# Step sizes by ScalarE's softplus between two table loads, and more products with C on VectorE, in a Mamba-style block with attention

## The chip, the cores and the metric

One NeuronCore of one Trainium2 chip runs the whole program. The metric is the device time of one execution in microseconds (us). The five engines run their own instruction streams in order: TensorE (PE in the profile), VectorE (DVE), ScalarE (ACT), GpSimd (POOL) and SyncE (SP), whose queue issues the DMAs. They wait for each other on semaphores.

## What is computed

The input is eight images of 96 channels by 64 by 64 points. For each image the reference does a layer norm, a projection to 192 channels, a depthwise convolution and a SiLU; then four selective scans over 4096 points each (two orders of reading the image, each forwards and backwards); then a norm, a gate, a projection, two 3x3 convolutions with GELU, an attention without softmax and a small feed-forward net. The change lies in the scans, cut here to what matters:

```python
delta = softplus(dts + dt_projs_b)            # step sizes, 192 channels x 4096 points, for each of 4 directions
def step(hst, inp):                           # hst: 192 channels x 16 states
    u_i, dt_i, b_i, c_i = inp
    dA = exp(dt_i[..., None] * A)             # decays
    hst = dA * hst + (dt_i * u_i)[..., None] * b_i
    y = einsum('bkdn,bkn->bkd', hst, c_i)     # products with C, summed over the 16 states
    return hst, y
```

## The kernel before

**Units and slots.** The scans are cut into 256 units: 8 images x 4 directions x 8 chunks of T = 512 points. A unit holds 192 channels x 16 states x 512 points, as 24 tiles of 128 x 512. They are worked in 24 slots, six groups n = 0 to 5 of four slots each. Per slot, ScalarE makes one tile of decays into PSUM (`decays`, L1123, an Exp), and VectorE runs one scan instruction over 512 points (L1195). `decays(q + 2)` is issued in slot q, so the decays of a slot are issued two slots ahead of its scan. Four PSUM banks hold decays. GpSimd makes the inputs of a whole group at once (`inputs`, L998, 128 x 2048: step size times u, times B). TensorE sums the products over the states (`sums`, L1024).

**Products with C.** Where a slot is "banked", the scan is written over its decays in PSUM, and VectorE multiplies it by C in a further instruction (L1201), issued after the next slot's scan; ScalarE copies the last column as the carry (L1202). In the other slots the scan is written over the inputs in SBUF; ScalarE copies the carries of the whole group at once after its last slot (L1207), and GpSimd multiplies what is not banked of the group by C (`outputs`, L1004). `BANKED` (L34) gives how many of the four slots of each group are banked: (4, 0, 4, 0, 4, 2) in 56 units, (4, 0, 4, 0, 4, 3) in 200.

**Step sizes.** `step_sizes` (L953) makes softplus(x) = max(x, 0) + ln(1 + exp(-|x|)) in steps: the matmul that makes x in PSUM (L963), then Abs, Exp and Ln on ScalarE (L971, L973, L975), then maximum and sum on VectorE (L977), then step size times u on GpSimd (L980). One unit needs one such tile for channels 0 to 127 ("a"), and two neighbouring units share one for channels 128 to 191 ("b"), so two units need three. They are made one unit ahead or two, in slots written out by hand in `plan` (L1057): tile "a" in slots 6, 8, 9, 10, 11 and 12 of each unit, tile "b" in slots 9, 11, 12, 13, 15 and 16 of each odd unit. The PSUM banks "y01" and "y2" hold x, and also the sums over the states; `gather` (L1038) empties them by ScalarE in slots 3 and 7.

**Side streams.** Beside the scans of image b, the front of image b + 1 and the back end of image b - 1 advance by one step per slot or so (`Stream`, `advance`); their ScalarE, VectorE and TensorE instructions stand between those of the slots, in the order in which they are issued. SiLU and GELU need another activation table than Exp and Ln: `table` (L274) issues an ACT_TABLE_LOAD before and after them. `quiet` lets them in only in the slots listed in `CALM` (L267).

Within a slot the order of issue is: carry copies left from the slot before; decays of two slots on; the scan; the product of the slot before; the steps that `plan` put there; the side streams. Every engine works through its own share of that order.

Of the kernel before, what the change touches and what calls it, by code (L numbers as in the profile page):

```python
# [9 lines left out]
F32 = mybir.dt.float32  # L10
F16 = mybir.dt.float16
F8 = mybir.dt.float8e5
AF = mybir.ActivationFunctionType
ALU = mybir.AluOpType
# [5 lines left out]
B, C, HW = 8, 96, 64  # L20
L = HW * HW
DI, N, R = 192, 16, 6
T = 512
NC = L // T
G = 4
# [3 lines left out]
W2 = HW + 2  # L29
# [1 line left out]
SPREAD = 5  # L31
HB = 6

BANKED = ((4, 0, 4, 0, 4, 2), (4, 0, 4, 0, 4, 3))  # L34

HOLD = 3
LAND = 11
# [6 lines left out]
def kernel(ctx: ExitStack, tc: tile.TileContext, a, out):  # L44
# [8 lines left out]
    nc = tc.nc  # L53
    P = 128
# [8 lines left out]
    def bank(tag, name):  # L63
        return psum.tile([P, T], F32, tag=tag, name=name, bufs=BANKS[tag])
# [11 lines left out]
    one = const([P, 1], 1.0, "one")  # L76
# [110 lines left out]
    def back_kit(pool, tag, extra, other=None, upper=0):  # L187

        k = Kit()
        k.tag, k.solo, k.upper = tag, not extra, upper  # L190
        if other is None:
            k.ya, k.za, k.bs, k.r, k.d1, k.s1, k.s2, y, z = (plain(pool, f"{tag}b{i}") for i in range(9))
            k.pad = padded(pool, tag + "pad")
        else:
            k.ya, k.za = (x.t for x in other.x)
            k.bs, k.r, k.d1, k.s1 = other.e
            k.s2, y, z = (other.pre[:, i, :] for i in range(3))
            k.pad = other.pad
        k.yb, k.zb = Part(y), Part(z[64:P])
        k.ya, k.za, k.bs = Part(k.ya), Part(k.za), Part(k.bs)  # L200
        if pool is None:
            return k
        k.t2 = Part(k.r), k.ya
        k.ln = Part(pool.tile([C + 1, T], F32, name=tag + "ln"))
        nc.gpsimd.memset(k.ln.t, 1.0)
        k.im = other.im if other else Part(pool.tile([C + 1, 18, W2], F32, name=tag + "im"))
        k.m3 = [Part(pool.tile([C, 8, W2], F32, name=f"{tag}m3{i}")) for i in range(2)]
        k.gm = gm0 if not extra else pool.tile([P, 8, W2], F32, name=tag + "gm")
        if extra:
            nc.gpsimd.memset(k.gm, 0.0)  # L210
        k.x8 = pool.tile([C, T], F8, name=tag + "x8")
        k.h16 = pool.tile([P, 3, T], F16, name=tag + "h16")
        k.h8 = pool.tile([P, 3, T], F8, name=tag + "h8")
        k.o16 = pool.tile([C, T], F16, name=tag + "o16")
        return k
# [9 lines left out]
    def square(ap):  # L225
        return ap.rearrange("p (r w) -> p r w", r=8)
# [37 lines left out]

    alone = [False]
    place = [None]
    CALM = (0, 1, 8, 9, 16, 17)  # L267

    def quiet():

# [3 lines left out]
    def table(name):  # L274
        nc.scalar.preload_act_table_set(name)  # L275
# [457 lines left out]
    units, images = [], []  # L733
    for b in range(out.shape[0]):

        s = {"b": b, "done": set(), "live": b + 1 == out.shape[0], "pairs": (1, 0) if b else (0, 1)}
        images.append(s)
        for order, (pair, back) in enumerate((p, k) for p in s["pairs"] for k in range(2)):
            for i in range(NC):
                u = Unit()  # L740
                u.s, u.pair, u.back, u.k = s, pair, back, pair + 2 * back
                u.c, u.start = (NC - 1 - i if back else i), i == 0
                u.order, u.new, u.i = order, (order, i) == (0, 0), len(units)
                u.bc, u.hb, u.delta, u.du, u.p = {}, {}, {}, {}, {}
                u.banked = BANKED[int(b == 0 or u.i % 32 >= NC)]
                units.append(u)

    TILES = [(g, j) for g in range(2) for j in range(3)]
# [3 lines left out]
    first = front(0, images[0])  # L752
# [10 lines left out]
    dt_w = wp.tile([P, 3, 64], F32, name="dt_w")  # L763
# [161 lines left out]
    def states(u, what, g):  # L925

        t = sp.tile([P, G, T], F32, tag="bc"[what], name="bc"[what])
        r0 = u.back * (XD // 2) + what * N + g * 2 * G
        src = u.s["xd"][u.pair][u.c, r0 : r0 + 2 * G, :].rearrange("(h m) l -> h (m l)", h=2)
        for h in range(2):  # L930
            to = t[64 * h : 64 * h + 64].rearrange("p m l -> p (m l)")
            nc.sync.dma_start(to, src[h].unsqueeze(0).to_broadcast([64, G * T]))
        u.bc[what, g] = t
# [16 lines left out]
        for h, w in enumerate((u, v)):  # L950
            nc.sync.dma_start(u.ub[64 * h : 64 * h + 64], w.s["u"][w.pair][P:DI, bass.ts(w.c, T)])

    def step_sizes(us, i):  # L953

        u, which = us[0], "ab"[len(us) - 1]
        if i == 0:
            u.ps = bank("y01" if which == "a" else "y2", "dt")
            if which == "a":
                todo = [(u.ps, slice(0, P), u)]
            else:  # L960
                todo = [(u.ps[64 * h : 64 * h + 64], slice(P, DI), w) for h, w in enumerate(us)]
            for ps, d, w in todo:
                nc.tensor.matmul(ps, dt_w.rearrange("r j d -> r (j d)")[32 * w.k : 32 * w.k + R + 1, d], w.dts, start=True, stop=True)  # L963
            u.nat = sp.tile([P, T], F32, tag="nat" + which, name="nat", bufs=1)
            if which == "a":
                u.nata = u.nat
            else:
                for w in us:
                    w.natb = u.nat
        elif i == 1:  # L970
            nc.scalar.activation(u.nat, u.ps, AF.Abs)  # L971
        elif i == 2:
            nc.scalar.activation(u.nat, u.nat, AF.Exp, scale=-1.0)  # L973
        elif i == 3:
            nc.scalar.activation(u.nat, u.nat, AF.Ln, bias=one)  # L975
        elif i == 4:
            nc.vector.scalar_tensor_tensor(u.nat, u.ps, 0.0, u.nat, ALU.max, ALU.add)  # L977
        else:
            x = u.ua if which == "a" else u.ub
            nc.gpsimd.tensor_tensor(x, u.nat, x, ALU.mult)  # L980

    def spread(u, what, js):

# [16 lines left out]
    def outputs(u, n):  # L1000

        lo = u.banked[n]
        hb = u.hb[n][:, lo:, :]
        nc.gpsimd.tensor_tensor(hb, hb, u.bc[1, TILES[n][0]][:, lo:, :], ALU.mult)  # L1004

# [51 lines left out]
    def plan(u, last, nxt, third, fourth):  # L1057

        at = [[] for _ in range(24)]

        def put(slot, f, *args):
            at[slot].append((f, args))

        if last:
            put(0, outputs, last, 5)
            for m in range(2):
                put(m, sums, last, (3, 4), 2 + m)
            for m in range(2):
                put(3 + m, sums, last, (5,), m)
            put(3, gather, last, 0)  # L1070
            put(7, states, u, 1, 1)
            put(7, gather, last, 1)
        for n in range(6):
            to = (u, n + 2) if n < 4 else (nxt, n - 4)
            if to[0]:
                put(4 * n + 1, inputs, *to)
        if third and u.i % 2:
            put(16, step_sizes, (nxt, third), 5)
        put(8, outputs, u, 1)
        put(16, outputs, u, 3)  # L1080
        for m in range(4):
            put(13 + m, sums, u, (0, 1), m)
            if m < 2:
                put(18 + m, sums, u, (2,), m)
                put(22 + m, sums, u, (3, 4), m)
        put(18, before, u)
        if nxt:
            put(0, spread, nxt, 0, (0, 1))
            put(1, spread, nxt, 1, (0, 1))
            put(10, states, nxt, 0, 0)  # L1090
            put(15, states, nxt, 1, 0)
            put(20, states, nxt, 0, 1)
            if u.i % 2 == 0:
                put(15, spread, nxt, 0, (2,))
                put(16, spread, nxt, 1, (2,))
        if third:
            if third.i < NC:
                put(0, fetched_dt, third)
            put(5, fetched_u, third)
            for i, slot in enumerate((6, 8, 9, 10, 11, 12)):  # L1100
                put(slot, step_sizes, (third,), i)
            if u.i % 2:
                for i, slot in enumerate((9, 11, 12, 13, 15)):
                    put(slot, step_sizes, (nxt, third), i)
                put(17, spread, nxt, 0, (2,))
                put(18, spread, nxt, 1, (2,))
            elif u.i + 3 < len(units):
                put(21, fetched_pair, third, units[u.i + 3])
        if fourth and fourth.i >= NC:
            put(14, fetched_dt, fourth)  # L1110
        return at

    def at_index(i):
# [16 lines left out]
    fetched_u(units[0])  # L1130
    fetched_pair(*units[:2])
    states(units[0], 0, 0)
    for us, js in ((units[:1], (0, 1)), (units[:2], (2,))):
        for i in range(6):
            step_sizes(us, i)
        for what in range(2):
            spread(units[0], what, js)
    for what, g in ((1, 0), (0, 1), (1, 1)):
# [3 lines left out]
    inputs(units[0], 1)  # L1142
    decays(0)
    decays(1)
    for i in range(6):
        step_sizes(units[1:2], i)

    def advance(n):

# [4 lines left out]
    for u in units:  # L1154
        last, nxt, third, fourth = (at_index(u.i + d) for d in (-1, 1, 2, 3))
        if u.new:
            drained(*side)
            b = u.s["b"]
# [25 lines left out]
        for slot in range(24):  # L1184
            n, m = divmod(slot, G)
            g, j = TILES[n]
# [21 lines left out]
                )  # L1208
            for f, args in todo[slot]:
                f(*args)  # L1210
            place[0] = slot
            advance(slot)
    place[0] = None
    if product:
# [88 lines left out]
```

## Time and profile before

| | |
|---|---|
| median of 3 runs | 10769.33 us (10765.02 to 10771.17) |
| the profiled execution's own time | 10764.72 us |
| its span | 10763.0 us |
| first scan starts, last scan ends | 181 us, 10533 us |
| VectorE busy | 10158.1 us (94%) |
| GpSimd busy | 10118.0 us (94%) |
| TensorE busy | 8423.7 us (78%) |
| ScalarE busy | 7397.8 us (69%) |

An engine's busy time is the union of its instructions: neighbours overlap a little, so that the pitch from one start to the next is shorter than an instruction's duration. L12 is line 12 of the kernel. In a group of instructions the name before the arrow is what is written, the names behind it what is read; `x384` is the count; after it come the busy time in us, the mean ns of one, and after the bar the engine's idle time just before such instructions, with what ended most of it.

### The profile page before, as it was taken

Reading aid. Unit: us, or ns where it says so; the run is one execution under the profiler, and the core shown is the slowest. Engines: PE = TensorE matmul, PEld = TensorE weight load, DVE = VectorE, ACT = ScalarE, POOL = GpSimd, SP = SyncE. Lnnn points to the kernel's source line nnn. Section 1 sums busy time; section 2 is a strip of 40 time slices with the busy share of each in tenths; the row PEclk is TensorE's granted clock in tenths of the full one; section 3 lists DMA queues with packets and bytes.
Section 4 is the critical chain, followed back from the end, with each engine's and each line's share of the span. In section 5 each row is a group of like instructions: output and inputs, shape, how many; then the busy total and the mean of one; then the engine's idle time right before and its main releaser. Section 6 shows DMA issues by size and latency. Waiting matters only on the chain. (4 is left out here: it accounts for less than half of the span.)

```text
span 10763.0 us, 97608 instructions
## 1 busy us (share of the span) xinstructions
PE 8423.7 (78%) x23270; PEld 2274.2 (21%) x23270; DVE 10158.1 (94%) x11126; ACT 7397.8 (69%) x15154; POOL 10118.0 (94%) x2782
## 2 busy tenths in 40 slices
PE   7777668886788867888688886888768887677677
PEld 2121112221122211222122221222112221111112
DVE  3999999999999999999999999999999999999993
ACT  4666666777676776777767776677766767666674
POOL 3999999999999999999999999999999999999991
PEclk8888788987889878998789887898778987778788
DMA  6888888998889988898888988889888898888883
GB/s 148 208 205 209 200 209 214 226 226 200 215 216 227 227 193 220 216 231 219 201 218 214 237 212 202 217 220 237 198 211 218 219 235 200 202 203 210 208 214 94
DMA packets 1095381, 2253.29 MB, mean 209 GB/s; under 512 B 435993, under 2 KB 436698, under 8 KB 963731
## 3 DMA queue, kind: packets, MB, share of 16 engines
q1 hardware_dynamic: 1094803, 2247.05, 84.5%
q8 instruction: 184, 3.01, 0.1%
q14 instruction: 394, 3.23, 0.1%
HBM read 1507.14 MB, written 336.69 MB: 171 GB/s over the span
## 5 line engine op out<-in xcount | busy, mean ns | idle before, releaser
L998 POOL TENSOR_TENSOR hb<-b,du 128x2048 f32<-128x2048 f32 x1536 | 6952.6, 4546 | 6.1 <-DMA du<-ua 5.2
L1024 PE MATMUL p<-hb,halves 128*64 128x512 f32 x12288 | 3713.8, 707 | 1053.0 <-POOL hb L1004 562.6
L1123 ACT ACTIVATE da<-delta,w_a_logs 128x512 f32<-128x512 f32 x6144 | 4164.3, 689 | 541.5 <-DVE hb L1195 447.5
L1195 DVE TENSOR_TENSOR_SCAN da<-da,carry,hb 128x512 f32<-128x512 f32 x3311 | 4164.0, 1274 | 90.7 <-ACT carry L1202 37.0
L1004 POOL TENSOR_TENSOR hb<-hb,c 128x2048 f32<-128x2048 f32 (+2 forms) x768 | 2714.3, 3534 | 222.3 <-ACT carry L1207 203.0
L1195 DVE TENSOR_TENSOR_SCAN hb<-da,carry,hb 128x512 f32<-128x512 f32 x2065 | 2547.0, 1265 | 1.8
L1201 DVE TENSOR_TENSOR hb<-da,c 128x512 f32<-128x512 f32 x3784 | 2534.0, 670 | 1.8 <-DMA c<-xd 0.9
L1202 ACT COPY carry<-da 128x1 f32<-128x1 f32 x3784 | 593.8, 157 | 2054.5 <-DVE hb L1201 2045.1
L1024 PEld LDWEIGHTS p<-hb,halves 128*64 128x64 f32 x12288 | 904.8, 157 | 3697.8 <-issue 1876.0
L313 PE MATMUL conv<-f0im,taps 97*128 97x512 f32 (+1 forms) x2088 | 867.7, 655 | 37.2 <-ACT f0pre L369 32.2
L1195 DVE TENSOR_TENSOR_SCAN da<-da,hb 128x512 f32<-128x512 f32 x473 | 566.1, 1214 | 28.0 <-POOL hb L998 26.6
L963 PE MATMUL dt<-dts,dt_w 7*128 7x512 f32 (+1 forms) x1024 | 485.9, 742 | 92.3 <-ACT carry L1207 36.2
L980 POOL TENSOR_TENSOR ua<-nat,ua 128x512 f32<-128x512 f32 x256 | 329.9, 1289 | 170.9 <-DVE nat L977 161.8
L313 PEld LDWEIGHTS conv<-f0im,taps 97*128 97x128 f32 (+1 forms) x2088 | 256.4, 173 | 588.2 <-issue 508.8
L1207 ACT COPY carry<-hb 128x4 f32<-128x4 f32 (+2 forms) x768 | 149.7, 195 | 302.1 <-DVE hb L1195 293.7
L1195 DVE TENSOR_TENSOR_SCAN hb<-da,hb 128x512 f32<-128x512 f32 x295 | 346.8, 1205 | 1.7 <-ACT carry L1202 1.7
L259 PE MATMUL var<-f1e,ones_c 96*96 96x512 f32 x350 | 225.6, 731 | 121.8 <-ACT f1e L256 68.5
L253 PE MATMUL ctr<-f1e,cen_c 96*96 96x512 f32 x402 | 218.1, 649 | 86.1 <-ACT f1e L592 34.2
L977 DVE SCALAR_TENSOR_TENSOR nat<-dt,nat 128x512 f32<-128x512 f32 x384 | 258.0, 672 | 17.9 <-ACT nat L975 12.7
L975 ACT ACTIVATE nat<-nat,one 128x512 f32<-128x512 f32 x384 | 271.8, 708 | 0.1
L497 PE MATMUL cab<-f1im,cab_w 97*32 97x512 f32 x1044 | 256.0, 603 | 12.5 <-DMA f1im<-xld 7.1
L275 ACT ACT_TABLE_LOAD x193 | 247.6, 1283 | 4.1 <-PEq L1292 0.8
(430 smaller groups left out, 7586.0 us busy)
## 6 DMA issues: line engine op xcount, KB each, us to landing
b<-xd SPq DMA_DIRECT2D x1024, 512.0 KB
c<-xd SPq DMA_DIRECT2D x1024, 512.0 KB
delta<-nat SPq DMA_DIRECT2D x1536, 128.0 KB
du<-ua SPq DMA_DIRECT2D x1024, 128.0 KB
y<-yt SPq DMA_DIRECT2D x512, 256.0 KB
u<-y SPq DMA_DIRECT2D x384, 256.0 KB
ua<-u SPq DMA_DIRECT2D x256, 256.0 KB
du<-ub SPq DMA_DIRECT2D x512, 128.0 KB
```

Source lines behind the costliest of these rows:

```text
L313: nc.tensor.matmul(ps, taps[:, t, lo : lo + n], im[:, r0 + dy : r0 + dy + 8, dx : dx + HW], start=t == 0, stop=t == 8,)
L963: nc.tensor.matmul(ps, dt_w.rearrange("r j d -> r (j d)")[32 * w.k : 32 * w.k + R + 1, d], w.dts, start=True, stop=True)
L975: nc.scalar.activation(u.nat, u.nat, AF.Ln, bias=one)
L977: nc.vector.scalar_tensor_tensor(u.nat, u.ps, 0.0, u.nat, ALU.max, ALU.add)
L980: nc.gpsimd.tensor_tensor(x, u.nat, x, ALU.mult)
L998: nc.gpsimd.tensor_tensor(hb, u.bc[0, g], u.du[j].unsqueeze(1).to_broadcast([P, G, T]), ALU.mult)
L1004: nc.gpsimd.tensor_tensor(hb, hb, u.bc[1, TILES[n][0]][:, lo:, :], ALU.mult)
L1024: nc.tensor.matmul(ps, halves, u.hb[n][:, i, :], start=TILES[n][0] == 0 and m == 0, stop=False, skip_group_check=True)
L1123: nc.scalar.activation(da[q], u.delta[j], AF.Exp, scale=a_neg[:, u.k, j, g * G + m : g * G + m + 1])
L1195: nc.vector.tensor_tensor_scan(dd if banked else x, dd, x, 0.0 if u.start else col, ALU.mult, ALU.add)
L1201: nc.vector.tensor_tensor(x, d, c, ALU.mult)
L1202: kept.append(lambda: nc.scalar.copy(col, d[:, at : at + 1]))
```

## The change

`step_sums` issues the matmuls of x, and `steps_made` runs one Softplus of ScalarE from PSUM to SBUF in place of Abs, Exp, Ln and VectorE's step. All three tiles of two units are made together: in each even unit, `begun` issues the matmuls of the first "a" tile and of the "b" tile in slot 8, and `ended` issues in slot 9 a table load, Softplus of the first tile, the matmul of the second "a" tile (the bank "y01" holds only one), Softplus of the "b" tile, Softplus of the second "a" tile, and the load of the old table. GpSimd's multiplication by u is put in the slots where it was. The tiles `nat` have two buffers each, and the second convolution's `m3` of the back end shares memory with another tile that was there. `CALM` now counts the 48 slots of an even and an odd unit, and the slots 8 and 9 of even units are no longer in it. `BANKED` is (4, 0, 4, 0, 4, 3), and (4, 0, 4, 0, 4, 4) in every fourth unit of the first image and of the directions but the first of the others. The rows for the matmul (`fetched_dt`) are loaded for two units at once.

```diff
-BANKED = ((4, 0, 4, 0, 4, 2), (4, 0, 4, 0, 4, 3))
+BANKED = ((4, 0, 4, 0, 4, 3), (4, 0, 4, 0, 4, 4))
...
-    CALM = (0, 1, 8, 9, 16, 17)
+    CALM = (0, 1, 16, 17, 24, 25, 32, 33, 40, 41)
...
-                u.banked = BANKED[int(b == 0 or u.i % 32 >= NC)]
+                u.banked = BANKED[int((b == 0 or u.i % 32 >= NC) and u.i % 4 == 0)]
...
-        elif i == 1:
-            nc.scalar.activation(u.nat, u.ps, AF.Abs)
-        elif i == 2:
-            nc.scalar.activation(u.nat, u.nat, AF.Exp, scale=-1.0)
-        elif i == 3:
-            nc.scalar.activation(u.nat, u.nat, AF.Ln, bias=one)
-        elif i == 4:
-            nc.vector.scalar_tensor_tensor(u.nat, u.ps, 0.0, u.nat, ALU.max, ALU.add)
...
+        nat = sp.tile([P, T], F32, tag="nat" + which, name="nat")
+        nc.scalar.activation(nat, ps, AF.Softplus)
...
+    def step_sizes(u, v):
+
+        first, both = (step_sums(us) for us in ((u,), (u, v)))
+
+        def made():
+            table("softplus")
+            steps_made((u,), first)
+            second = step_sums((v,))
+            steps_made((u, v), both)
+            steps_made((v,), second)
+            table("natural_log_exp_and_others")
+
+        return made
...
@@ outputs
+        if lo == G:
+            return
...
@@ plan
-            for i, slot in enumerate((6, 8, 9, 10, 11, 12)):
-                put(slot, step_sizes, (third,), i)
+            put(12, scaled_input, (third,))
             if u.i % 2:
-                for i, slot in enumerate((9, 11, 12, 13, 15)):
-                    put(slot, step_sizes, (nxt, third), i)
                 put(17, spread, nxt, 0, (2,))
                 put(18, spread, nxt, 1, (2,))
-            elif u.i + 3 < len(units):
-                put(21, fetched_pair, third, units[u.i + 3])
-        if fourth and fourth.i >= NC:
+            else:
+                if third.i < NC:
+                    put(0, fetched_dt, third)
+                    put(0, fetched_dt, fourth)
+                put(8, begun, third, fourth)
+                put(9, ended, third)
+                put(21, fetched_pair, third, fourth)
+        if u.i % 2 and fourth and fourth.i >= NC:
             put(14, fetched_dt, fourth)
+            put(14, fetched_dt, units[fourth.i + 1])
...
-            place[0] = slot
+            place[0] = slot + 24 * (u.i % 2)
```

## The prediction

> **What bounds the kernel now.** I read the busy times first, then the windows of the steady images, the waits of VectorE and GpSimd there, the groups that the edit touches, and last the timeline of a place where a bracket of table loads already stands in slot 9 of an even unit.
>
> ```profile
> 2950.00:4250.00 1300.00, 1043.12 (x2908) 277.02 (x2906) 1264.17 (x1377) 924.86 (x1899) 1264.69 (x345) 0.85 0.88 216
> ```
>
> This is a window of 1300 us: PE, its weight loads, VectorE, ScalarE, GpSimd. VectorE and GpSimd are both busy for 97.3%, ScalarE for 71%. Two units take 2 x (10533 - 181) / 256 = 80.9 us over the whole scan and 80.1 us in such windows; each of the two engines is idle for some 2.2 us of that. Which one waits for the other shows in the waits between 2950 and 9450 us (total us, times, longest):
>
> ```profile
> DVE da L1195 <- POOL hb L998: 30.8, 36, 2.1
> DVE da L1195 <- ACT carry L1202: 30.6, 15, 3.2
> ...
> POOL hb L1004 <- ACT carry L1207: 141.9, 113, 2.9
> ```
>
> GpSimd's idle time is almost wholly the wait for the carry copy behind scan 7, which is a wait for VectorE. VectorE waits for GpSimd little. So VectorE sets the pace, with GpSimd some 1 us per unit short of it, and a stall of VectorE is paid.
>
> **What goes and comes.** The groups (times, busy us, mean ns):
>
> ```profile
> L977 DVE SCALAR_TENSOR_TENSOR nat<-dt,nat 128x512 f32<-128x512 f32 x384 | 258.0, 672 | 17.9 <-ACT nat L975 12.7 <-ACT carry L1202 4.5
> ...
> L1201 DVE TENSOR_TENSOR hb<-da,c 128x512 f32<-128x512 f32 x3784 | 2534.0, 670 | 1.8 <-DMA c<-xd 0.9
> ...
> L275 ACT ACT_TABLE_LOAD x193 | 247.6, 1283 | 4.1 <-PEq L1292 0.8
> L973 ACT ACTIVATE nat<-nat 128x512 f32<-128x512 f32 x384 | 237.5, 618 | 0.1
> L971 ACT ACTIVATE nat<-dt 128x512 f32<-128x512 f32 x384 | 222.9, 580 | 36.4 <-PE dt L963 35.9
> ```
>
> - VectorE loses L977. Its price is its pitch, 0.60 us (below: a product at 599.06 and the next scan at 599.65 show 0.59 for the like of it). 381 of the 384 lie beside scans: 381 x 0.60 = 229 us less.
> - VectorE gains products. Before: 56 x 14 + 200 x 15 = 3784. After: 256 x 15 + 50 = 3890, since 50 of the 200 units are every fourth. That is 106 (0.41 per unit), at 0.59: 63 us more. Net for VectorE: -166 us, or -1.3 us per pair of units.
> - GpSimd: 56 outputs of 1024 shrink to 512 (2362 - 1291 ns by their groups: 60 us), 50 of 512 vanish (1.22 us pitch: 61 us). Together -121 us, -0.95 per pair. It isn't the pacer, so by itself this brings nothing; it keeps GpSimd behind VectorE in every case: 77.9 - 0.95 = 77.0 busy in a pair that lasts at least 78.8.
> - ScalarE loses 1152 instructions, 732 us, and gains 384 Softplus at the 0.58 us of Abs, which also reads PSUM (223 us), and 256 table loads at 1.30 us pitch (333 us): 176 us less in sum. But 127 times in the loop it now does all of that in one piece, while it makes no decays.
> - At nothing: GpSimd's multiplications (same slots), the DMAs for the rows (as many, issued half a unit or more ahead of slot 8; SP's queue is passed by two issues together instead of one and one), the shared memory of `m3` (other stages), `CALM` (only two of the bracketed SiLUs and GELUs of the scan loop begin in slots 8 or 9 of an even unit), the three tiles ahead of the loop.
>
> **The bracket of slot 9, the one cost.** This is a SiLU of the front that happened to be let in at slot 9 of an even unit:
>
> ```profile
> 595.53 1.26 DVE L1195 TENSOR_TENSOR_SCAN hb<-da,carry,hb 128x512 f32<-128x512 f32 x1
> ...
> 597.28 0.69 ACT L1123 ACTIVATE da<-delta,w_a_logs 128x512 f32<-128x512 f32 x1
> ...
> 597.91 0.58 ACT L971 ACTIVATE nat<-dt 128x512 f32<-128x512 f32 x1
> ...
> 598.38 0.68 ACT L1123 ACTIVATE da<-delta,w_a_logs 128x512 f32<-128x512 f32 x1
> ...
> 599.62 1.28 ACT L275 ACT_TABLE_LOAD   x1
> ...
> 600.91 1.48 ACT L321 ACTIVATE f0pre<-f0pre 128x1536 f32<-128x1536 f32 x1
> ...
> 602.41 1.28 ACT L275 ACT_TABLE_LOAD   x1
> ...
> 602.62 0.67 DVE L1201 TENSOR_TENSOR hb<-da,c 128x512 f32<-128x512 f32 x1
> 603.71 0.16 ACT L1202 COPY carry<-da 128x1 f32<-128x1 f32 x1
> 603.90 0.69 ACT L1123 ACTIVATE da<-delta,w_a_logs 128x512 f32<-128x512 f32 x1
> ...
> 605.26 0.69 DVE L977 SCALAR_TENSOR_TENSOR nat<-dt,nat 128x512 f32<-128x512 f32 x1 [1.97 <-ACT carry L1202]
> ```
>
> Scan 7 ends at 596.79. ScalarE can't be earlier than that, since the carry copy of group 1 stands ahead of decay 10. Then come decays 10 and 11 and the bracket, and decay 12 only behind it. VectorE has scans 8 to 11 and products 8 to 10 to go on with, which end at 603.29; it sat idle for 1.97 us.
>
> The table load costs its 1.28 us here: the next instruction starts 0.01 us behind its end, twice. The Trainium skill ("ScalarE: Activation LUTs", section "What ACT_TABLE_LOAD costs") adds a drain of about 1.38 us to every switch. By it, 127 brackets would cost 127 x 2 x 1.38 = 350 us on top, an estimate from that page; the row shows no such drain and decides.
>
> The same path for the new bracket, in means over the 125 even units 2 to 250, counted along the trace from the end of scan 7. ScalarE: decay 11 ends at 2.70, less Abs 0.58: 2.12. Table load 1.30; Softplus 0.58; the third Softplus must wait for the matmul of the second "a" tile, which can't start before the first Softplus has emptied its bank: 1.12 (L963, two passes) and 0.06 for each hand-over, 1.24, which covers the "b" Softplus; Softplus 0.58; table load 1.30; side-stream instructions there 0.17; carry copy 0.17; decay 12 0.69. Sum 8.15 us. VectorE: scan 12 starts at 7.40, less L977's 0.60 and little else: 6.75. The stall is 1.40 us. I add 0.35: TensorE is sometimes late (L971 waited for it 33 times in 384, 1.1 us each), ScalarE now has no lead behind the bracket, so a side instruction of 0.6 to 1.5 us in the next slots stalls VectorE again, and side operations of VectorE wait for ScalarE's evictions. Taken: s = 1.75 us.
>
> Bounds of s. Low, 0.7: the stall may stand in place of VectorE's waits for GpSimd (62.9 us in all, 0.5 per bracket), and ScalarE gives back 0.2 in odd units, where six instructions leave it. High, 2.7: Softplus at the 0.71 of Ln, TensorE late by a side matmul (0.7) each time, and no absorption.
>
> **The sum**, against the profiled execution's 10764.7: 127 x 1.75 = 222; 222 - 166 = +56: 10821. The median of the runs is 4.6 above that execution: 10825. With s = 0.7: 89 - 166 = -77, 10692. With s = 2.7: 343 - 166 = +177, 10946. It breaks even at 166 / 127 = 1.31 us.
>
> **The rivals.**
> - *The cover is long enough (faster).* Place: between scan 7 and scan 12 of even units. It decides from s under 1.31, and beyond the 0.2% (21.5 us, about what can be told from no change) from s under 1.14. At s = 0.9 it gives -52: 10717. For it: brackets of 3.3 to 4.1 us in slots 16, 25 and 40 left VectorE idle for 0.07 to 0.4 us in the mean. Against it: this one lasts 5.0 us, and the four old ones in slots 8, 9, 32 and 33 left 1.5 to 2.0.
> - *GpSimd is the pacer after all (faster).* Then VectorE's stall hides in its waits, and the 121 us of GpSimd count: 10648. Against: 142 us of waits for VectorE against 31.
> - *It evens out (no change).* s between 1.14 and 1.48: 10769.
> - *A long bracket (slower still).* Softplus takes longer than any of the three it replaces, a drain shows, or TensorE is regularly late: s above 2.7, say 3.3: 419 - 166 = +253, 11022.
>
> That the edit doesn't do what it says is small: 0.41 products per unit, not 0.45, a matter of 6 us.
>
> **The numbers.** Forecast (s from 1.48 to 2.7) 0.52; cover long enough 0.20; GpSimd the pacer 0.07; even 0.13; long bracket 0.08. Faster 0.27, same 0.13, slower 0.60. The range 10690 to 10950 takes in the bounds of s and leaves out the second and the last rival. The forecast alone would hold 10791 to 10950.
>
> **What would show it.** Right: 449 table loads at 1.28 us; Softplus rows near 0.58 us; between the first and the third some 0.65 us in which ScalarE waits for L963's matmul; VectorE idle before scan 12 of nearly every even unit for 1 to 2 us, put down to ScalarE's decays or carry copy, 150 to 250 us in all; VectorE busy for 9990 us, GpSimd for 9997, ScalarE for 7220; GpSimd's wait for carry copies grows. Wrong: VectorE's idle time before scan 12 under 1 us, or a stall of the same size with GpSimd, not VectorE, without idle time; a gap behind the table loads; products other than 3890.

## The result, and the profile after

The changed kernel takes 10945.17 us in the median (10939.24 to 10951.28), against 10767.17 us for the kernel before: a ratio of 1.0166, 95% interval 1.0148 to 1.0183. The change costs 178 us, where the forecast was 56. It lies inside the range, on the forecast's side, but at three times its size.

The same window of the steady images, with the columns as before (PE, weight loads, VectorE, ScalarE, GpSimd):

```profile
2950.00:4250.00 1300.00, 1047.66 (x2859) 280.78 (x2860) 1220.52 (x1318) 900.66 (x1808) 1226.07 (x334) 0.84 0.87 212
```

VectorE and GpSimd have both fallen from 97% to 94%: they do less, and wait more. The totals of the page say how exactly the work was foreseen: VectorE 9994.5 us (forecast 9990), GpSimd 9995.7 us (9997), 3890 products, 449 table loads. ScalarE's 7322 us lies 100 above its forecast, largely because the 1152 instructions taken away overlapped with their neighbours, by 141 us in all along the trace, and were priced with their full durations.

```profile
L1226 DVE TENSOR_TENSOR hb<-da,c 128x512 f32<-128x512 f32 x3890 | 2617.8, 673 | 2.1 <-DMA c<-xd 1.2
...
L279 ACT ACT_TABLE_LOAD x449 | 576.1, 1283 | 8.5 <-PEq L1317 0.8
...
L973 ACT ACTIVATE nat<-dt 128x512 f32<-128x512 f32 x384 | 217.7, 596 | 284.1 <-PE dt L966 281.4
```

The third line is the news. A Softplus takes 0.596 us, as hoped, but ScalarE sat idle for 284 us ahead of them, waiting for the matmul of L966: 2.2 us for each of the 127 brackets. The waits of VectorE and GpSimd between 2950 and 9450 us:

```profile
DVE hb L1220 <- ACT carry L1227: 205.7, 64, 7.8
DVE da L1220 <- ACT carry L1227: 44.4, 20, 3.2
...
POOL hb L1029 <- ACT carry L1232: 325.7, 147, 5.7
```

The first line is scan 12 behind the bracket. In the kernel before, the like of it was next to nothing:

```profile
DVE hb L1195 <- ACT carry L1202: 1.4, 5, 0.3
```

Counted along the whole scan loop, VectorE is idle for 601 us instead of 261, and 432 of that lies in slots 8 to 15 of even units, where it was 30. Slot 12 alone has 343 us, or 2.70 per bracket, where it had nothing. GpSimd's wait for the carry copies grows from 142 to 326 us: it stands behind VectorE.

One bracket in the timeline (start, us, what):

```profile
5602.12 2.44 DVE L1220 TENSOR_TENSOR_SCAN da<-da,carry,hb 128x512 f32<-128x512 f32 x2
...
5602.37 1.97 PE L966 MATMUL dt<-dts,dt_w 7*64 7x512 f32 x4 [5.25 <-ACT yt L1074]
...
5603.70 1.28 ACT L279 ACT_TABLE_LOAD   x1
...
5605.00 1.08 ACT L973 ACTIVATE nat<-dt 128x512 f32<-128x512 f32 x2
...
5605.65 2.07 PE L966 MATMUL dt<-dts,dt_w 7*128 7x512 f32 x2 [1.31 <-ACT nat L973]
...
5607.76 0.60 ACT L973 ACTIVATE nat<-dt 128x512 f32<-128x512 f32 x1 [1.67 <-PE dt L966]
5608.02 0.68 DVE L1226 TENSOR_TENSOR hb<-da,c 128x512 f32<-128x512 f32 x1
5608.37 1.28 ACT L279 ACT_TABLE_LOAD   x1
...
5609.66 0.16 ACT L1227 COPY carry<-da 128x1 f32<-128x1 f32 x1
5609.86 0.69 ACT L1149 ACTIVATE da<-delta,w_a_logs 128x512 f32<-128x512 f32 x1
...
5610.65 1.28 DVE L1220 TENSOR_TENSOR_SCAN hb<-da,carry,hb 128x512 f32<-128x512 f32 x1 [1.95 <-ACT carry L1227]
```

The second matmul starts 0.06 us behind the first Softplus, as assumed, but takes 2.07 us and not 1.12. The granted TensorE clock is at half here: the two records that this matmul leaves last 1.21 and 1.06 us, where brackets with the full clock show 0.69 and 0.59. The clock was at half in 114 of 127 brackets when this matmul started, and in 120 when the second of its records did; the counts of brackets below are made at that second record. Nothing is seen behind the table loads: where the next instruction has nothing to wait for, it follows within 0.02 us, as before.

### The profile page after: what moved, and what is told of

It reads as the page before. It is cut to its first block, busy times and chain, and to the rows that moved or that the text cites. A ratio compares the mean times of both kernels' runs of the same rounds, so it can differ in the third digit from the quotient of the medians.

```text
span 10937.7 us, 96398 instructions
## 1 busy us (share of the span) xinstructions
PE 8624.2 (79%) x23270; PEld 2331.7 (21%) x23270; DVE 9994.5 (91%) x10848; ACT 7322.4 (67%) x14698; POOL 9995.7 (91%) x2732
## 5 line engine op out<-in xcount | busy, mean ns | idle before, releaser
L1220 DVE TENSOR_TENSOR_SCAN da<-da,carry,hb 128x512 f32<-128x512 f32 x3385 | 4270.7, 1277 | 76.7 <-ACT carry L1227 52.5
L1029 POOL TENSOR_TENSOR hb<-hb,c 128x2048 f32<-128x2048 f32 (+1 forms) x718 | 2580.2, 3594 | 521.0 <-ACT carry L1232 484.1
L1220 DVE TENSOR_TENSOR_SCAN hb<-da,carry,hb 128x512 f32<-128x512 f32 x1991 | 2457.4, 1268 | 285.0 <-ACT carry L1227 269.7
L1226 DVE TENSOR_TENSOR hb<-da,c 128x512 f32<-128x512 f32 x3890 | 2617.8, 673 | 2.1 <-DMA c<-xd 1.2
L966 PE MATMUL dt<-dts,dt_w 7*64 7x512 f32 (+1 forms) x1024 | 584.6, 837 | 301.0 <-ACT nat L973 158.5
L1220 DVE TENSOR_TENSOR_SCAN da<-da,hb 128x512 f32<-128x512 f32 x505 | 605.8, 1216 | 37.6 <-POOL hb L1021 31.5
L973 ACT ACTIVATE nat<-dt 128x512 f32<-128x512 f32 x384 | 217.7, 596 | 284.1 <-PE dt L966 281.4
L1220 DVE TENSOR_TENSOR_SCAN hb<-da,hb 128x512 f32<-128x512 f32 x263 | 308.7, 1208 | 66.2 <-ACT da L1149 37.2
L1232 ACT COPY carry<-hb 128x4 f32<-128x4 f32 (+1 forms) x718 | 140.5, 196 | 325.4 <-DVE hb L1220 311.2
L538 PE MATMUL cab<-f1pre,cab_w 96*96 96x512 f32 x348 | 213.7, 733 | 78.3 <-ACT f1e L547 48.3
```

Source lines behind the costliest of these rows:

```text
L966: nc.tensor.matmul(to, dt_w.rearrange("r j d -> r (j d)")[32 * w.k : 32 * w.k + R + 1, d], w.dts, start=True, stop=True)
L1220: nc.vector.tensor_tensor_scan(dd if banked else x, dd, x, 0.0 if u.start else col, ALU.mult, ALU.add)
L1226: nc.vector.tensor_tensor(x, d, c, ALU.mult)
```

## The experiments

Times are medians; each ratio is to the kernel before on the same chip (10763 to 10767 us), with its 95% interval. "Idle by slot" is VectorE's idle time in the scan loop, counted along the trace.

**The third Softplus without its wait.**

```diff
-            second = step_sums((v,))
+            second = first
```

> The third Softplus reads the first tile's bank again; the matmul of the second "a" tile is left out, so the step sizes of every second unit are those of the unit before. Theory A (the wait for that matmul, 1.9 us between the second and the third Softplus in the mean, is the mis-sized term): the bracket falls from 6.5 to some 4.5 us, VectorE's idle time in slots 8 to 15 of even units from 402 to some 150 us, the time from 10945 to some 10700 us, below the kernel before. Theory B (the two table loads and the cover alone make the stall, and what is taken away here comes back in the next wait): above 10880 us.

10767.8 us (1.0005, 0.9995 to 1.0014): 177 us less than the changed kernel, and level with the kernel before. The bracket falls from 6.5 to 4.35 us in the mean, VectorE's idle time in slots 8 to 15 of even units from 432 to 177 us. VectorE's waits between 2950 and 9450 us, first for the carry copies ahead of scan 12, then for GpSimd's inputs:

```profile
DVE hb L1220 <- ACT carry L1227: 66.4, 64, 3.1
DVE da L1220 <- POOL hb L1021: 52.0, 34, 4.5
```

Theory A is borne out in its cause: without the wait for the second matmul, as much time comes back as the change had lost. But its 10700 us is missed by 68. Of the 255 us that VectorE's idle time in these slots loses, part turns into waits elsewhere: slots 0 and 24, where VectorE waits for GpSimd's inputs, rise from 14 to 80 us. So there was something else wrong in the sum, too.

**No table loads.** Both `table` calls of the bracket are taken out, and Softplus becomes Abs.

> The two table loads are left out and Softplus is replaced by Abs, which every table has; the step sizes are then |x|. Theory A: the bracket loses 2 x 1.30 us, some 0.3 us of which comes back because the second instruction meets its matmul earlier; 127 x 2.3 = 290 us: 10655 us, with the wait for the second matmul of 1.9 us left as it is. Theory C (the loads are hidden behind the wait for TensorE, since the matmuls need that time anyway): above 10850 us.

10799.9 us (1.0035, 1.0022 to 1.0048), 145 us less than the changed kernel: half of what A expected, and more than C allowed. The time from the end of scan 7 to the start of scan 12 falls from 10.08 to 7.88 us, 2.2 us for 2.6 us of loads; the wait for the second matmul stays at 1.9 us. As in the run above, not all of a local gain arrives at the end. The loads and the wait are no separate parts of the loss: 145 and 177 us together are more than the bracket costs in all (248 us, worked out below).

**The products back to GpSimd.**

```diff
-BANKED = ((4, 0, 4, 0, 4, 3), (4, 0, 4, 0, 4, 4))
+BANKED = ((4, 0, 4, 0, 4, 2), (4, 0, 4, 0, 4, 3))
```

(with the old choice between the two)

> The changed kernel with the banked slots of the kernel before: 106 products go back to GpSimd. If VectorE is still the pacer, its 106 x 0.59 = 63 us come off: 10880 us. If GpSimd has become the pacer: 121 us more, 11065 us.

10916.5 us (1.0142, 1.0125 to 1.0158), 29 us less than the changed kernel, which the two intervals barely tell apart: VectorE's side of the question, but under half of its price. VectorE's busy time falls by 66 us, and its idle time in the loop rises from 601 to 634.

**TensorE kept at work ahead of the bracket.** The first tile's matmul is issued in slot 5 and again in 6, 7 and 8, the "b" tile's in 8 and 9.

> TensorE is kept at work ahead of the bracket: the first tile's matmul is issued in slot 5 and written again in slots 6, 7 and 8, the "b" tile's in slots 8 and 9. Theory A1 (the second matmul takes 2.07 instead of 1.12 us because the granted clock is halved at that moment, after TensorE had little to do): its clock is full in most brackets, it takes 1.1 us there, and up to 127 x 0.95 = 120 us come off: 10830 to 10880 us. Theory A2 (it is slow for what it is, a single matmul with seven rows behind a weight load): still 2.07 us, and the time is the same or up to 60 us longer because side matmuls stand behind the added ones.

11475.0 us (1.0656, 1.0638 to 1.0675). Far outside both expectations: the added matmuls ran at the half clock themselves, so that the "b" tile came late (the second Softplus waited for 3.2 us in the mean). The clock at the second matmul was at half in 126 of 127 brackets. Being busy is not what kept the clock up: TensorE was busy for 93 to 98% of slots 5 to 8 of even units, and the share of the full clock fell from 0.88 to 0.42 over them. This run doesn't tell whether the seven rows were the reason.

**The rows of the array.** Six matmuls into the first tile's bank in slots 5 to 7, ahead of its own, with 128 rows in one kernel and with seven in the other:

```diff
+        for _ in range(2):
+            nc.tensor.matmul(u.first, ident, now.bc[0, 1][:, 0, :], start=True, stop=True)      # e11
+            nc.tensor.matmul(u.first, dt_w...[32 * u.k : 32 * u.k + R + 1, 0:P], u.dts, ...)     # e12 in its place
```

> In slots 5, 6 and 7 two matmuls each with 128 rows and 128 columns of weights (the identity on a tile of B) are issued into the first tile's bank, ahead of its own matmul, which overwrites them. Theory A1 (the granted clock follows how much of the array works, and seven rows count for little): the second matmul finds the full clock in over half of the 127 brackets, where the changed kernel has it in 7; it takes 1.1 us there. Theory A2 (the clock falls for another reason, whatever TensorE does): full clock in under 20. The time also pays for the matmuls that now stand ahead: 10850 to 11050 us.

> The same six matmuls in the same slots with seven rows, the first tile's own matmul over and over. Theory A1: the clock at the second matmul stays halved in over 100 of 127 brackets, as in the changed kernel, though TensorE is as busy in instructions as with 128 rows. Theory A2: no difference between the two. Time 10950 to 11250 us.

11118.6 us (1.0326, 1.0311 to 1.0342) with 128 rows, 11915.3 us (1.1063, 1.1047 to 1.1080) with seven; both are longer than expected. The groups of e11, the added ones first, then the first tile's own matmul and the "b" tile's:

```profile
L998 PE MATMUL dt<-b,ident 128*128 128x512 f32 x1524 | 713.6, 605 | 20.5 <-ACT carry L1236 11.4 <-ACT yt L1081 9.1
...
L1001 PE MATMUL dt<-dts,dt_w 7*128 7x512 f32 x254 | 142.3, 640 | 0.0
L966 PE MATMUL dt<-dts,dt_w 7*64 7x512 f32 x512 | 137.6, 613 | 0.0
```

and those of e12:

```profile
L998 PE MATMUL dt<-dts,dt_w 7*128 7x512 f32 x1524 | 1060.2, 846 | 26.8 <-ACT carry L1236 11.1 <-ACT yt L1081 9.1 <-DMA dts<-xd 6.6
...
L966 PE MATMUL dt<-dts,dt_w 7*64 7x512 f32 x512 | 246.0, 1057 | 0.0
L1001 PE MATMUL dt<-dts,dt_w 7*128 7x512 f32 x254 | 242.8, 1056 | 0.0
```

The same count, columns and places, and in slots 6 to 8 TensorE is busy for 97% or more in both. Behind 128 rows a record of the same seven-row matmul takes 640 ns, behind seven rows 1056. Full clock at the second matmul: 76 of 127 brackets against 3. A1 holds for the clock. The two kernels differ in the values multiplied, too; rows and values were not told apart. Neither run is faster, since six matmuls stand ahead of the "b" tile's; in e11 the first Softplus starts 2.63 us behind decay 11 instead of 1.48. So the runs show the clock's effect on the matmul, but none shows the time with the clock alone put right.

**The bracket a slot later.** `put(10, ended, third)` for `put(9, ended, third)`.

> The bracket of the changed kernel is issued in slot 10 instead of slot 9, behind decay 12. Theory A (the stall is the bracket less what VectorE has in stock when it begins): the stock is a scan and a product more, a decay and a carry copy less, 0.8 us per bracket: 127 x 0.8 = 100 us less, 10845 us. Theory D (the unbanked slots 12 to 15, short for VectorE, take the cover back): 10920 to 10980 us.

10941.9 us (1.0163, 1.0148 to 1.0178): no change. The stall is the same size and has only moved to slots 12 and 13 (76 and 273 us, before 343 and 1). Theory D named the right outcome, but the trace shows another reason. Decay 12 ends 2.84 us behind scan 8 (2.81 in odd units, which have no bracket), since it needs the PSUM bank of slot 8, which is free only when product 8 has been made; the stock of decays at the bracket's start is bounded by the four banks.

**Two brackets instead of one.** Even units make their "a" tile and the "b" tile, odd units their "a" tile:

```diff
-                put(8, begun, third, fourth)
-                put(9, ended, third)
+            put(8, begun, *((third,) if u.i % 2 else (third, fourth)))
+            put(9, ended, third)
```

> Every unit has its own bracket: even units make their "a" and the shared "b" tile, odd units their "a" tile alone; no Softplus waits for a bank any more, at the price of two more table loads for two units. Theory A (a bracket is covered up to some 4 us, and the wait for the second matmul was what broke the cover): brackets of 3.7 and 3.2 us, VectorE idle for some 0.9 us in even and 0.5 us in odd units there: 127 x 1.4 = 178, less 166 and less some 60 that the changed kernel saved elsewhere: 10690 to 10760 us. Theory B (each table load is paid): 254 more loads at 1.3 us against 127 x 1.9 us of wait saved: 11030 us.

10769.2 us (1.0002, 0.9993 to 1.0012), 9 us above A's range and far from B: 254 more table loads, and still 176 us less than the changed kernel. VectorE's idle time in slots 8 to 15 is 115 us in even and 82 in odd units. The brackets last 3.91 and 3.35 us in the mean; such a bracket is nearly covered.

**The products alone, in the kernel before.**

> The kernel before with the banked slots of the changed one, nothing else: 106 products more on VectorE, 121 us less on GpSimd. If VectorE is the pacer of the kernel before, as the prediction had it: 106 x 0.59 = 63 us more, 10830 us. If GpSimd is: 121 us less, 10646 us. If the two pace each other, in between: 10740 to 10790 us.

10792.0 us (1.0026, 1.0017 to 1.0035): 27 us more, neither 63 nor -121, and 2 us above the range for two engines that pace each other, which it fits best.

**VectorE's step taken away without a bracket.** In the kernel before, Exp from PSUM, then Ln with a bias of one; Abs and the maximum with the sum are gone:

```diff
-            nc.scalar.activation(u.nat, u.ps, AF.Abs)
...
-            nc.scalar.activation(u.nat, u.nat, AF.Exp, scale=-1.0)
+            nc.scalar.activation(u.nat, u.ps, AF.Exp)
...
-            nc.vector.scalar_tensor_tensor(u.nat, u.ps, 0.0, u.nat, ALU.max, ALU.add)
```

> The kernel before without VectorE's step and without a bracket: softplus(x) as ln(1 + exp(x)), by Exp from PSUM in the slot where Exp was, and Ln; Abs and VectorE's maximum and sum are gone. It is the same function as long as exp(x) stays finite; products as before. It prices what the change set out to remove. If VectorE is the pacer, all of 381 x 0.60 = 229 us comes off: 10540 us. If the two pace each other, about half: 10640 to 10700 us. If GpSimd is the pacer, nothing: 10760 us.

10674.4 us (0.9911, 0.9897 to 0.9926), the fastest of all: 90 us less, of the 229 that VectorE no longer works.

> The same with the banked slots of the changed kernel: VectorE at -229 + 63 = -166 us, GpSimd at -121 us, no bracket. This is the sum of the prediction with a stall of nothing: 10600 us if VectorE is the pacer. If GpSimd held e13 back, it is faster than e13; if VectorE did, 63 us slower.

10697.1 us (0.9936, 0.9920 to 0.9953): 68 us less than before, 23 more than with the old products. Two of its VectorE waits between 2950 and 9450 us, and one of GpSimd:

```profile
DVE da L1193 <- POOL hb L994: 52.0, 50, 2.2
DVE da L1193 <- ACT carry L1200: 39.2, 20, 3.2
...
POOL hb L1002 <- ACT carry L1205: 194.8, 101, 4.6
```

Busy time falls by 147 us, idle time in the loop rises from 261 to 332. The wait for GpSimd's inputs has grown from 31 us, and GpSimd's wait behind VectorE from 142: each waits more for the other. This is the prediction's sum with a stall of nothing, measured: -68, not -166. Both kernels hold only where exp(x) is finite, which is so for this input (x lies between -37 and -11).

## Why the prediction was right or wrong

**Right:** the direction and the place of the loss. The bracket in slot 9 of even units outlasts VectorE's stock of decays, and scan 12 waits. The work moved was counted to 5 us of VectorE's and 1 us of GpSimd's busy time. That a table load costs 1.28 us and hides no drain held: behind 424 of the 449 the next instruction starts within 0.02 us, and behind the other 25 it waits for TensorE or a DMA. On this the Trainium skill ("ScalarE: Activation LUTs", section "What ACT_TABLE_LOAD costs") differs from the measurement.

**Wrong in size, in three terms.** The runs split the 178 us, in the order of the table; the prediction's parts are regrouped in the same way.

| term | predicted | measured, and by what |
|---|---|---|
| VectorE's net work, -166 | -166 | -68: e14 against the kernel before |
| the bracket without the wait | 1.03 x 127 = +131 | +71: e1 (10768) against e14 (10697) |
| the wait for the second matmul | 0.72 x 127 = +91 | +177: the changed kernel against e1 |
| sum | +56 | +180, measured +178 |

The 0.72 is the prediction's 1.24 us less the 0.52 us of the "b" Softplus that it lets run meanwhile. The measured terms are differences between runs, mostly on different chips; by the intervals above each is uncertain by some 20 us. Another order would split the bracket otherwise, as the run without loads shows.

*The step "1.12 (L963, two passes)".* The price is that of this row of the kernel before, a matmul issued for slot 6:

```profile
592.67 1.12 PE L963 MATMUL dt<-dts,dt_w 7*128 7x512 f32 x2
```

The granted clock was full there. The price had to be that of slot 10. The kernel before shows it, counted by slot: the full clock holds for 0.75 of slot 6 of even units, but for 0.37 of slot 10 and 0.33 of slot 11. By the kernel's order the sums with 128 rows stop at slot 4 and start again at slot 13, and TensorE's busy share falls from 0.76 in slot 6 to 0.39 in slot 11; which of the two weighs more in this kernel was not tried. At half clock the matmul takes 2.07 us, and it starts 0.43 us later than assumed in the mean: in 29 of 127 brackets other matmuls, mostly of the side streams, stood ahead of it. From the end of the first Softplus to the start of the third it was 2.54 us instead of 1.24. The rest of the path was right: decay 11 ended at 2.15 us (2.12), and third Softplus, load, copies and decay took 2.9 (2.9). Only the first Softplus waited for 0.18 more, for its matmul, and scan 12 started 0.4 behind decay 12. VectorE itself came some 0.6 us later, largely since it had already waited in slots 9 and 11.

*The step "VectorE sets the pace, ... and a stall of VectorE is paid".* It led to counting all 166 us freed as time. That GpSimd waited for VectorE for 142 us, and VectorE for GpSimd for 31, showed who waits now; it didn't show that 1.3 us per pair could be given away before the other becomes late. By GpSimd's order within a unit (inputs two groups ahead, products behind the carry copies) each waits for the other at fixed points. The products alone show the lower price: 106 of them cost 27 us in the kernel before and 29 in the changed one, not 63; of the two, the 27 is clear of the noise. In the terms of the rivals, the second ("GpSimd is the pacer after all") held in part, which I had made an either-or.

*The stall, s = 1.40 + 0.35 = 1.75 us.* The idle time before scan 12 is 2.70 us per bracket. With that, the prediction's sum gives 127 x 2.70 - 166 = +177 us, next to the measured 178. In the scan loop VectorE's busy time falls by 162 us; its idle time grows by 343 us in slot 12 and by 59 in the rest of slots 8 to 15 of even units, and falls by 58 elsewhere; the loop takes 182 us longer. But this adds up what VectorE did, and doesn't tell what a shorter stall would save. By the runs the whole bracket costs 71 + 177 = 248 us, or 1.95 each and not 2.70, because some of VectorE's idle time there stands in place of waits that the freed time brings in anyway, at slots 0 and 24 (54 us before, 83 in e14, 14 in the changed kernel). That 1.95 lies near 1.75 is a cancellation: the wait cost twice its price, the rest of the bracket half. And it is luck that the high bound, s = 2.7, gives the measured time: it stood on a Softplus at 0.71 us, which took 0.596, and on a side matmul of 0.7 us each time, where the late start came to 0.43; the clock was not in it.

*Two smaller readings.* A pair of units takes 81.2 us in the steady windows, not 80.1; GpSimd's time in a pair is then 79.0 less 0.95, against 79.9, and still the shorter. And the 1.97 us of VectorE in the older bracket ended with L977, which needed the Ln of L975 (ready at 605.23); decay 12 was ready at 604.59, 1.3 us behind the last product. The sum used neither the 80.1 nor the 1.97.

**Open:** which of GpSimd's order, its buffers and ScalarE's carry copies turns VectorE's freed time into waits in e13 and e14 was not tried.

## What to carry to other kernels

An instruction that must wait for a matmul inside a closed bracket is priced by TensorE's clock at that place and by what stands ahead in its queue, so read the granted clock by position in the loop and not from a row of the same instruction elsewhere. Where two engines are busy for 97% each, work taken off one can be worth less than its time (here some 0.4 of it), whichever of the two waits for the other at present: price it between nothing and all. And where a bracket must close out other work, two short ones without a wait inside can be cheaper than one long one, even with twice the table loads.

## What the runs showed of the hardware

Seven-row matmuls didn't keep TensorE's clock up. The Trainium skill ("TensorE: Matmul & The Clock Gate", section "Part 1: The HAM clock gate (the "warmup" mystery)") says that the gate opens when TensorE has been busy for some 3.4 us and closes when idle. In e12 TensorE was busy for 97 to 99% of slots 6 to 8 of even units, with 128 columns but seven rows, and the share of the full clock fell from 0.76 to 0.30 over them, and to 0.05 in slot 10, busy throughout; in e11, with as many matmuls at 128 rows, it was 0.99 or more in all three. In these runs the share of the time alone doesn't account for the clock; the rows at work do, if the values multiplied, which differ too, play no part. A matmul of 512 float32 columns with seven rows takes 1.12 us from start to end at the full clock and 2.07 at half.
